# Experts' remainders of at most 64 rows in tiles of 320 rows, with column-halved output products

## The chip, the cores and the metric

The kernel runs on one core of a Trainium2 chip. The metric is device time in microseconds (us) of one launch; lower is better. Three runs of the kernel before gave 2270.71, 2273.41 and 2272.79 us (median 2272.79).

The engines are named as the profile names them: PE (TensorE matmul), PEld (its weight loads), DVE (VectorE), ACT (ScalarE), POOL (GpSimd) and SP (SyncE, which here only issues DMAs).

## The reference, cut to what matters

The input `x` has 4 images of 256 channels and 32x32 pixels. A first layer (normalisation, four small state-space scans, convolutions, attention, a projection) updates it; then each of the 4096 pixels is a token of 256 numbers that goes to two of eight experts. Only that second layer is touched by the change:

```python
top_w, top_i = jax.lax.top_k(gate_logits, TOP_K)          # TOP_K = 2 of 8 experts
top_w = jax.nn.softmax(top_w, axis=-1)
for e in range(E):
    h = jax.nn.gelu(xf @ W1[e] + b1[e], approximate=False)  # 256 -> 1024
    out = out + w_dense[:, e:e + 1] * (h @ W2[e] + b2[e])   # 1024 -> 256
```

There are 2 x 4096 = 8192 rows of work. Evaluated on its own inputs, the reference sends experts 0 to 7 these numbers of rows: 1024, 1065, 1023, 1012, 1006, 1048, 1041, 973. Divided by 256, that is 4, 4, 3, 3, 3, 4, 4, 3 full tiles and remainders of 0, 41, 255, 244, 238, 24, 17, 205 rows.

## The kernel before, in words

**Order of the whole.** The instruction order of all engines is written out by a hand-made scheduler: Python generators are advanced in ticks, and each `yield` gives way to the others. Image by image the first layer runs; when an image has passed it, `dispatch` normalises its tokens, picks the experts and scatters the rows into an array `XS` in device memory, in which each expert owns a region. Expert tiles (the generator `tiles()` and the class `Experts`) run beside the last image's convolutions and normalisations and then alone to the end.

**Tiles of rows.** A normal tile takes T = 256 rows of one expert. A wide tile (series WIDE = 3) takes 384: the last full 256 rows of an expert and the up to 128 rows that remain behind them. Which expert and which first row a tile has is computed on DVE from the counts (`wide_series`, `series`, `table`) and read into registers that address the DMAs. The code is laid out for the worst case: `SERIES = (8, 8, 19, 8)` tiles in four series. The last `LATE` = 7 normal tiles and the last `LATE_WIDE` = 4 wide ones stand in a conditional block behind everything else (`run`, line 2052) that is entered only if the counts need one of them. The tiles that always run are 8 + 8 + 12 normal and 4 wide. After the first 16 normal ones, the order is wide, normal, normal, normal, four times over.

**An expert must fit.** An expert whose remainder is at most 128 has it taken along by a wide tile; a larger remainder takes a padded normal tile of its own. Free wide slots take another expert's tile.

**One tile, step by step.** While tile n runs, tile n+1 is prepared. SP issues the DMA of its rows (`rows`, line 2069: `xs`, as 128-row blocks beside each other) and of its weights (`load`, lines 2095 to 2100: W1 and W2 in four pieces of 512 KB, biases). In the middle of tile n, behind its first output block, `front` turns the rows: PE transposes of 128x128 (line 2118, `xp`), a DVE copy out of PSUM (line 2121, `xT`), and four small DVE operations that make each row's weight and destination (lines 2126 to 2133). Then `tile` computes:

- the hidden layer, line 2149: 8 pieces of 128 hidden units, each two products (two halves of the 256 input channels) that stream `xT` past a piece of W1. Every fp32 product is two passes in the trace, so a tile has 32 matmul instructions of 256 columns, or of 384 in a wide tile;
- Gelu on ACT, line 2154, into `hs`;
- the output, line 2161: for each block of 128 rows, 8 products that hold 128 rows of `hs` as weights and stream W2 (256 columns), so 16 instructions of 256 columns a block. Two blocks share a PSUM tile, so that a wide tile's third block has one for itself;
- the bias on DVE (line 2170), the routing weight on DVE (line 2175), and one indirect DMA a block that adds the rows into `Y` (POOL, line 2181).

At the very end `bring_back` reads `Y`, transposes it and writes the output.

Of the kernel before, what the change touches and what calls it, by code (L numbers as in the profile page):

```python
# [9 lines left out]
F32 = mybir.dt.float32  # L10
# [35 lines left out]

LATE, LATE_WIDE = 7, 4


LOG_EXP = "natural_log_exp_and_others"
# [20 lines left out]
def network(  # L73
# [71 lines left out]
    with tc.tile_pool(name="w_conv", bufs=1) as wp, tc.tile_pool(  # L145
# [1149 lines left out]
        def tiles():  # L1295
# [45 lines left out]
            def rows(n):  # L1341
                s, i = order[n]
                xs[n] = act4.tile(
                    [P, experts.width(s) // P, experts.ROW], F32, tag="a4", name=f"xs_{n}"
                )
                experts.rows(s, i, tables[s], xs[n])

# [27 lines left out]
            for n in range(len(order)):  # L1375
                while n not in got or len(got[n]) == 4:
                    ahead(n, NHC)
                    yield 4
                if order[n] in ((0, 2), (1, 2)):
                    experts.count_up(order[n][0] + 1, temp)  # L1380
                if order[n] == (rest - 1, 2):
                    experts.count_up(wide, temp)
                while not T.get(("scanned",)):
                    yield 1
                while T.get(("hold",)):
                    T["held",] = True
                    yield 1
                s = order[n][0]
                pieces = 2 if s == wide else 1
                hs = [  # L1390
                    act8.tile(
                        [P, NHC // pieces, experts.width(s)], F32, tag="a8", name=f"hs_{n}_{k}"
                    ) for k in range(pieces)
                ]
                for at, _ in enumerate(experts.tile(
                    n, s, got[n], hs,
                    act4.tile([P, experts.width(s) // P, C], F32, tag="a4", name=f"ys_{n}"),
                )):
                    if at < 4:
                        loaded[0] = None  # L1400
                    ahead(n + 1, at)
                    yield T.get(("pace",), 1)
# [134 lines left out]
class Experts:  # L1537
# [10 lines left out]

    T = 256

    SERIES = (8, 8, 19, 8)
    WIDE = 3
    NT = N // P
    ROW = C + 4
# [2 lines left out]
    def __init__(self, ctx, tc, psum, B, b1, ident, eps5, ones_mean, Wg, bg, W1, W2, b2, out):  # L1557
# [3 lines left out]
        self.B = B  # L1561
        T, NT = self.T, self.NT
        NTOK = self.NTOK = B * N
        self.NTILE = max(NTOK * 2 // T + k - -(-k * (T // 2 + 1) // T) for k in range(NE + 1))
        PITCH = self.PITCH = NTOK + T + P
        self.SPARE = NE * PITCH
        md = ctx.enter_context(
# [298 lines left out]

    def width(self, s):

        return self.T + P if s == self.WIDE else self.T

    def follow(self, ins, others, reason):
        kind = mybir.DependencyInfo(
# [5 lines left out]
    def count_up(self, s, temp):  # L1878

        nc, K, n = self.nc, self.NTOK // self.T, self.SERIES[s]  # L1880
        steps = temp(f"steps_{s}", [P, NE, K])
        base = {self.WIDE: 0, self.WIDE - 1: self.T // 2}.get(s, self.T - 1)
        nc.gpsimd.iota(
            steps, [[0, NE], [self.T, K]], base=base,
            channel_multiplier=0, allow_small_or_imprecise_dtypes=True,
        )
        which = temp(f"which_{s}", [P, n, NE])
        nc.gpsimd.iota(
            which, [[1, n], [0, NE]], base=0, channel_multiplier=0,
            allow_small_or_imprecise_dtypes=True,  # L1890
        )
        self.numbers[s] = steps, which
# [131 lines left out]
    def run(self, tables):  # L2024

        tc, nc = self.tc, self.nc
        with tc.tile_pool(name="moe2", bufs=2) as m2:
            def load(v):
                return nc.values_load(
                    v[0:1, 0:1], min_val=0, max_val=sum(self.SERIES),  # L2030
                    skip_runtime_bounds_check_because="made from counts of at most NTOK rows",
                )

            def late_tile(s, i):
                j, W = f"{s}_{i}", self.width(s)
                w1 = m2.tile([P, NC2, DFF], F32, tag="w1", name=f"w1_{j}")
                w2 = m2.tile([P, NHC, C], F32, tag="w2", name=f"w2_{j}")
                got = self.load(
                    s, i, tables[s], [w1], [w2], m2.tile([P, C], F32, tag="b2", name=f"b2_{j}")
                )  # L2040
                xs = m2.tile([P, W // P, self.ROW], F32, tag="xs", name=f"xs_{j}")
                self.rows(s, i, tables[s], xs)
                got += self.front(
                    j, s, i, tables[s], xs, m2.tile([P, NC2, W], F32, tag="xT", name=f"xT_{j}")
                )
                for _ in self.tile(
                    j, s, got, [m2.tile([P, NHC, W], F32, tag="hs", name=f"hs_{j}")],
                    m2.tile([P, W // P, C], F32, tag="ys", name=f"ys_{j}"),
                ):
                    pass  # L2050

            with tc.If(load(self.any_late) > 0):
                for s, late in ((self.WIDE - 1, LATE), (self.WIDE, LATE_WIDE)):
                    n = self.SERIES[s]
                    with tc.If(load(self.used[s]) > 0):
                        for i in range(n - late, n):
                            late_tile(s, i)
            for b in range(self.B):
                self.bring_back(b, m2)

    def rows(self, s, i, table, xs):

        nc, tc, T = self.nc, self.tc, self.width(s)
        row = nc.values_load(
            table[1][0:1, 1, i : i + 1], engines=[mybir.EngineType.SP], min_val=0,
            max_val=self.SPARE,
            skip_runtime_bounds_check_because="made from counts of at most NTOK rows",
        )
        ins = nc.sync.dma_start(xs, self.XS[ds(row, T), :].rearrange("(t p) c -> p t c", p=P))
        if self.image_of(s) + 1 < self.B:  # L2070
            here = self.sent_by[self.image_of(s)]
            for other in self.sent[here:]:
                tc.declare_no_dep(ins.ins, other.ins, reason="full tiles of earlier images")
            self.read.append(ins)
        else:
            here = len(self.sent)
        if i == 0:
            self.follow(ins, self.sent[:here], "all rows are in")

    def load(self, s, i, table, w1, w2, b2_s):  # L2080

# [26 lines left out]
    def front(self, j, s, i, table, xs, xT):  # L2108

        nc, psum, m0, W = self.nc, self.psum, self.m0, self.width(s)  # L2110
        nt = W // P
        expert, _ = table
        each = NC2 if NC2 * W <= HALF else 1
        for c0 in range(0, NC2, each):
            xp = psum.tile([P, HALF], F32, tag="ps", name=f"xp_{j}_{c0}")
            for t in range(nt):
                for c in range(each):
                    nc.tensor.transpose(  # L2118
                        xp[:, ds(c * W + t * P, P)], xs[:, t, ts(c0 + c, P)], self.ident
                    )  # L2120
            nc.vector.tensor_copy(  # L2121
                xT[:, ds(c0, each), :].rearrange("p c t -> p (c t)"), xp[:, 0 : each * W]
            )

        late = m0.tile([P, 3, 1], F32, tag="late", name=f"late_{j}", bufs=2)[:, 0:nt]
        nc.vector.tensor_scalar(
            late, xs[:, :, C + 3 : C + 4], expert[:, i, :], None, ALU.is_equal
        )
        wgt = m0.tile([P, 3, 1], F32, tag="wgt", name=f"wgt_{j}", bufs=4)[:, 0:nt]
        nc.vector.tensor_tensor(wgt, late, xs[:, :, C + 2 : C + 3], ALU.mult)  # L2130
        nc.vector.tensor_tensor(wgt, wgt, xs[:, :, C + 1 : C + 2], ALU.add)
        dest = m0.tile([P, 3, 1], mybir.dt.int32, tag="dest", name=f"dest_{j}", bufs=4)[:, 0:nt]
        nc.vector.tensor_copy(dest, xs[:, :, C : C + 1])
        return [xT, wgt, dest]

    def tile(self, j, s, got, hs, ys):

        nc, psum, W = self.nc, self.psum, self.width(s)
        w1, w2, b2_s, b1_s, xT, wgt, dest = got
        nt, each, piece = W // P, max(1, HALF // W), NHC // len(hs)  # L2140

        def hidden(k):
            return hs[k // piece][:, k % piece, :]
# [1 line left out]
        for k0 in range(0, NHC, each):  # L2145
# [8 lines left out]
                nc.scalar.activation(hidden(k), hp[:, i, :], AF.Gelu, bias=b1_s[:, 0, k : k + 1])  # L2154
            if k0 % 2 == 0:
                yield
        for t in range(nt):
            if t % 2 == 0:
                yp = psum.tile([P, HALF], F32, tag="ps", name=f"y_{j}_{t}")
            for k in range(NHC):  # L2160
                nc.tensor.matmul(  # L2161
                    yp[:, ts(t % 2, C)], hidden(k)[:, ts(t, P)], w2(k),
                    start=(k == 0), stop=(k == NHC - 1),
                )
                if k % 4 == 3:
                    yield
            if t % 2 or t == nt - 1:
                t0 = t - t % 2
                some = t + 1 - t0
                nc.vector.tensor_tensor(  # L2170
                    ys[:, t0 : t + 1], yp[:, 0 : some * C].rearrange("p (t c) -> p t c", t=some),
                    b2_s.rearrange("p (a c) -> p a c", a=1).to_broadcast([P, some, C]), ALU.add,
                )
        for t in range(nt):
            nc.vector.tensor_scalar(ys[:, t, :], ys[:, t, :], wgt[:, t, :], None, ALU.mult)  # L2175

        added = []
        for t in range(nt):
            if t:
                nc.gpsimd.memset(self.apart, 0.0)  # L2180
            ins = nc.gpsimd.indirect_dma_start(  # L2181
                out=self.Y[:, :],
                out_offset=bass.IndirectOffsetOnAxis(ap=dest[:, t, :], axis=0),
                in_=ys[:, t, :], in_offset=None, compute_op=ALU.add,
            )
            for other in added:
                self.tc.declare_no_dep(ins.ins, other.ins, reason="no two share a row")
# [126 lines left out]
```

## Time and profile before

| | |
|---|---|
| median of three runs | 2272.79 us (2270.71 to 2273.41) |
| profiled execution, its own time | 2272.61 us |
| its span, first to last instruction | 2270.8 us |
| mean granted PE clock | 0.947 of full |
| PE busy | 2005.6 us (88%) |
| DVE / ACT / POOL busy | 1531.8 / 1234.5 / 1046.4 us |
| hidden layer of a normal tile (32 passes of 256 columns), last stretch | 6.91 us |
| hidden layer of a wide tile (32 passes of 384 columns) | 10.32 us |
| output of one block (16 passes of 256 columns) | 3.45 us |
| indirect adds into `Y` | 68 |

The span is cut into 40 slices for the busy shares; one slice is 56.8 us. A matmul row `128*64 128x512` gives the part of the array (rows x columns) that holds weights, then the moving operand (partitions x columns). PE is pipelined: the duration of one matmul is longer than the distance to the next, so costs are read from distances between starts.

### The profile page before, as it was taken

The page shows a single profiled execution, that of the slowest core. Times are in us where ns is not written, and L with a number is a line of the kernel's source. Part 1 is how long each engine was busy: PE and PEld are TensorE (multiplying, and loading weights), DVE is VectorE, ACT ScalarE, POOL GpSimd, SP SyncE. Part 2 cuts the span into 40 slices and gives each one's busy share as a digit, 9 for nine tenths or more (in the row PEclk, how much of TensorE's full clock was granted, in tenths as well). Part 3 has the DMA queues.
Part 4 walks back from the last instruction along what each step waited for, and adds up shares of the span by engine and source line. Part 5 has one row for each costly group of instructions (what it writes and reads, how often), then busy time and mean ns, then how long its engine had stood idle before and what let it go on. Part 6 is the DMA issues. An engine that isn't in the chain of part 4 may idle for free. (4 is left out here: it accounts for less than half of the span.)

```text
span 2270.8 us, 28249 instructions
## 1 busy us (share of the span) xinstructions
PE 2005.6 (88%) x8742; PEld 889.8 (39%) x8742; DVE 1531.8 (67%) x2211; ACT 1234.5 (54%) x2301; POOL 1046.4 (46%) x930
## 2 busy tenths in 40 slices
PE   6777878999987999987789999659999999999995
PEld 2111112322211332322123234116742677888884
DVE  3989998768899878789797977984245265111111
ACT  4665666678767666775746777325358432212221
POOL 0788888613688640576975034742040021422221
PEclk8889999999998999998899999789999999999997
DMA  3565553302453421244543013343240176866665
GB/s 100 142 155 121 124 137 89 99 10 69 100 128 93 98 48 38 76 106 108 144 99 86 20 45 82 80 151 96 91 117 1 45 215 167 245 186 181 169 160 160
DMA packets 156814, 248.78 MB, mean 110 GB/s; under 512 B 34596, under 2 KB 101700, under 8 KB 156520
## 3 DMA queue, kind: packets, MB, share of 16 engines
q1 hardware_dynamic: 136032, 220.59, 36.2%
q0 software_dynamic: 12976, 17.58, 4.0%
q10 hardware_dynamic: 7640, 8.65, 1.2%
q8 instruction: 72, 1.18, 0.2%
q14 instruction: 94, 0.77, 0.1%
HBM read 135.39 MB, written 35.84 MB: 75 GB/s over the span
## 5 line engine op out<-in xcount | busy, mean ns | idle before, releaser
L698 POOL TENSOR_TENSOR dA<-hs,cs 128x512 f32<-128x512 f32 x512 | 684.3, 1344 | 430.6 <-DVE hs L690 294.7
L669 ACT ACTIVATE dA<-dts,A 128x512 f32<-128x512 f32 x512 | 358.8, 717 | 162.6 <-DMA dts<-dt 96.9
L2181 POOL DMA_INDIRECT Y<-ys,dest x68 | 109.6, 1612 | 535.1 <-DVE ys L2175 528.3
L708 PE MATMUL yp<-dA,quads 128*32 128x512 f32 x1024 | 277.4, 639 | 79.7 <-POOL dA L698 68.9
L2154 ACT ACTIVATE hs<-h,b 128x256 f32<-128x256 f32 (+1 forms) x256 | 112.1, 484 | 387.6 <-PE h L2149 273.6
L1053 ACT ACTIVATE e<-st 128x512 f32<-128x512 f32 x512 | 263.7, 605 | 102.5 <-PE st L1043 83.3
L679 DVE TENSOR_TENSOR dBu<-dts,bs 128x512 f32<-128x512 f32 x384 | 259.9, 678 | 85.4 <-PE bs L661 24.5
L2149 PE MATMUL h<-xT,w 128*128 128x256 f32 (+1 forms) x1024 | 249.3, 400 | 14.3 <-DVE xT L2121 14.3
L2161 PE MATMUL y<-w,hs 128*128 128x256 f32 x1088 | 248.9, 381 | 5.0 <-ACT hs L2154 5.0
L690 DVE TENSOR_TENSOR_SCAN hs<-dA,last,dBu 128x512 f32<-128x512 f32 x192 | 243.6, 1269 | 4.7 <-ACT sq_lgn L1135 1.3
L690 DVE TENSOR_TENSOR_SCAN hs<-dA,dBu 128x512 f32<-128x512 f32 x192 | 231.7, 1207 | 11.5 <-issue 4.4
L1099 DVE TENSOR_TENSOR e<-e,e 128x512 f32<-128x512 f32 x256 | 169.9, 725 | 84.5 <-ACT e L1053 46.4
L2149 PEld LDWEIGHTS h<-xT,w 128*128 128x128 f32 x1024 | 197.6, 194 | 66.5 <-DVE xT L2121 16.0
L2161 PEld LDWEIGHTS y<-w,hs 128*128 128x128 f32 x1088 | 205.2, 191 | 38.9 <-issue 6.1
L661 PE MATMUL bs<-u,xpwT_s 128*32 128x512 f32 x1024 | 169.4, 671 | 55.3 <-DVE hs L690 24.8
L2121 DVE COPY xT<-xp 128x512 f32<-128x512 f32 (+1 forms) x36 | 23.4, 659 | 274.6 <-PE xp L2118 262.1
L1043 PE MATMUL st<-qk 32*128 32x512 f32 x1024 | 176.7, 643 | 4.2 <-DVE ys L2170 2.6
L708 PEld LDWEIGHTS yp<-dA,quads 128*32 128x32 f32 x1024 | 49.2, 113 | 287.7 <-POOL dA L698 186.8
L1089 PE MATMUL av<-e,v 128*32 128x512 f32 x1024 | 139.3, 609 | 0.0
L1043 PEld LDWEIGHTS st<-qk 32*128 32x128 f32 x1024 | 60.3, 184 | 120.0 <-issue 87.3
L1063 PE MATMUL av<-e,every 128*32 128x512 f32 x512 | 87.5, 601 | 3.7 <-DVE e L1099 3.7
L679 DVE TENSOR_TENSOR bs<-dts,bs 128x512 f32<-128x512 f32 x128 | 86.1, 672 | 1.9 <-DMA dts<-dt 1.9
(319 smaller groups left out, 2706.4 us busy)
## 6 DMA issues: line engine op xcount, KB each, us to landing
dts<-dt SPq DMA_DIRECT2D x512, 128.0 KB
w<-in_W_dram SPq DMA_DIRECT2D x124, 512.0 KB
cs<-cd SPq DMA_DIRECT2D x512, 64.0 KB
xd<-xn SPq DMA_DIRECT2D x64, 128.0 KB
xs<-XS SPq DMA_DIRECT2D x28, 260.0 KB
xn<-in_x_dram SPq DMA_DIRECT2D x8, 512.0 KB
XL<-xl SPq DMA_DIRECT2D x8, 512.0 KB
xl<-XL SPq DMA_DIRECT2D x4, 1024.0 KB
```

Source lines behind the costliest of these rows:

```text
L661: nc.tensor.matmul(bs[r], xpwT_s[:, n, s : s + 1].to_broadcast([P, 32]), T[b, n, "u"][:, half(h)], start=True, stop=True,)
L669: nc.scalar.activation(dA, T[b, n, h, "dts", g][:, 0, :], AF.Exp, scale=A[:, g, n, q : q + 1])
L679: nc.vector.tensor_tensor(dBu, T[b, n, h, "dts", g][:, 1, :], T[b, n, h, "bs", q], ALU.mult)
L690: nc.vector.tensor_tensor_scan(hs, T[b, n, h, "dA", i], dBu, 0.0 if h == 0 else last, ALU.mult, ALU.add)
L698: nc.gpsimd.tensor_tensor(dA, hs, T[b, n, h, "cs", q], ALU.mult)
L708: nc.tensor.matmul(T[b, n, h, "yp"][ts(g, 32)], quads, T[b, n, h, "dA", q * GD + g], start=False, stop=(q == GS - 1),)
L1043: nc.tensor.matmul(sts[i], k[r, ts(kt, P)], q[r, half(h)], start=True, stop=not shifted)
L1053: nc.scalar.activation(es[i], sts[i], AF.Exp, scale=1.0 / HD**0.5)
L1089: nc.tensor.matmul(accs[0][ts(i, HD)], v8[:, kt, ts(4 * g + i, HD)], es[i], start=(kt == 0), stop=(kt == NK - 1),)
L1099: nc.vector.tensor_tensor(first[i], first[i], es[i], ALU.add)
L2149: nc.tensor.matmul(hp[:, i, :], w1(c, k0 + i), xT[:, c, :], start=(c == 0), stop=(c == NC2 - 1))
L2161: nc.tensor.matmul(yp[:, ts(t % 2, C)], hidden(k)[:, ts(t, P)], w2(k), start=(k == 0), stop=(k == NHC - 1),)
```

## The change

Wide tiles shrink from 384 to 320 rows (`REST = 64`). A remainder of up to 64 rows rides in a wide tile, a larger one takes a padded normal tile. The worst case needs more normal tiles for that, so the series becomes 21 long and 9 of it stand in the conditional block; the tiles that always run keep their number and order. A list `blocks(s)` replaces the count `W // P`: a wide tile has blocks of 128, 128 and 64 rows.

For the 64-row block each step has a form of its own:

- `rows` issues two DMAs for a wide tile, the full blocks and the 64 rows;
- `front` transposes 64 rows against a 64x64 identity, and issues its four small DVE operations twice;
- in `tile` the eight output products hold 64 rows of `hs` as weights, so half of the array's columns. Even pieces k go to columns and PSUM partitions 0 to 63, odd ones to 64 to 127: two partial sums beside each other. ACT then copies the upper partial sum to a tile `other`, DVE adds the bias to it, and DVE adds it to the lower one;
- weighting and the indirect add handle 64 rows.

```diff
-LATE, LATE_WIDE = 7, 4
+LATE, LATE_WIDE = 9, 4
+REST = 64
-    SERIES = (8, 8, 19, 8)
+    SERIES = (8, 8, 21, 8)
-        return self.T + P if s == self.WIDE else self.T
+        return self.T + REST if s == self.WIDE else self.T
+    def blocks(self, s):
+        W = self.width(s)
+        return [(t, min(P, W - t * P)) for t in range(-(-W // P))]
...
-        base = {self.WIDE: 0, self.WIDE - 1: self.T // 2}.get(s, self.T - 1)
+        base = {self.WIDE: 0, self.WIDE - 1: REST}.get(s, self.T - 1)
...
-        ins = nc.sync.dma_start(xs, self.XS[ds(row, T), :].rearrange("(t p) c -> p t c", p=P))
+        full = T // P
+        got = [
+            nc.sync.dma_start(
+                xs[:, 0:full], self.XS[ds(row, full * P), :].rearrange("(t p) c -> p t c", p=P)
+            )
+        ]
+        if T % P:
+            got.append(
+                nc.sync.dma_start(xs[0 : T % P, full], self.XS[ds(row + full * P, T % P), :])
+            )
...
-            for t in range(nt):
+            for t, n in blocks:
                 for c in range(each):
                     nc.tensor.transpose(
-                        xp[:, ds(c * W + t * P, P)], xs[:, t, ts(c0 + c, P)], self.ident
+                        xp[:, ds(c * W + t * P, n)], xs[0:n, t, ts(c0 + c, P)],
+                        self.ident[0:n, 0:n],
                     )
...
+        for n, ts_ in ((P, slice(0, full)), (W % P, slice(full, nt))):
+            if n:
+                x = xs[0:n, ts_]
+                nc.vector.tensor_scalar(
+                    late[0:n, ts_], x[:, :, C + 3 : C + 4], expert[0:n, i, :], None, ALU.is_equal
+                )
...
-        for t in range(nt):
+        for t, n in blocks:
             if t % 2 == 0:
                 yp = psum.tile([P, HALF], F32, tag="ps", name=f"y_{j}_{t}")
+            parts = P // n
             for k in range(NHC):
                 nc.tensor.matmul(
-                    yp[:, ts(t % 2, C)], hidden(k)[:, ts(t, P)], w2(k),
-                    start=(k == 0), stop=(k == NHC - 1),
+                    yp[ts(k % parts, n), ts(t % 2, C)], hidden(k)[:, ds(t * P, n)], w2(k),
+                    start=(k < parts), stop=(k >= NHC - parts),
                 )
                 if k % 4 == 3:
                     yield
-            if t % 2 or t == nt - 1:
+            if parts > 1:
+                other = m0.tile([REST, C], F32, tag="other", name=f"other_{j}", bufs=1)
+                nc.scalar.copy(other, yp[n:P, 0:C])
+                nc.vector.tensor_tensor(other, other, b2_s[0:n], ALU.add)
+                nc.vector.tensor_tensor(ys[0:n, t], yp[0:n, 0:C], other, ALU.add)
+            elif t % 2 or t == len(blocks) - 1:
...
-                out_offset=bass.IndirectOffsetOnAxis(ap=dest[:, t, :], axis=0),
-                in_=ys[:, t, :], in_offset=None, compute_op=ALU.add,
+                out_offset=bass.IndirectOffsetOnAxis(ap=dest[0:n, t, :], axis=0),
+                in_=ys[0:n, t, :], in_offset=None, compute_op=ALU.add,
```

More of the change, by code (lines that the diff above doesn't have):

```diff
@@ L1343, in rows @@
                 xs[n] = act4.tile(
-                    [P, experts.width(s) // P, experts.ROW], F32, tag="a4", name=f"xs_{n}"
+                    [P, len(experts.blocks(s)), experts.ROW], F32, tag="a4", name=f"xs_{n}"
                 )
@@ L1396, in tiles @@
                     n, s, got[n], hs,
-                    act4.tile([P, experts.width(s) // P, C], F32, tag="a4", name=f"ys_{n}"),
+                    act4.tile([P, len(experts.blocks(s)), C], F32, tag="a4", name=f"ys_{n}"),
                 )):
@@ L1563, in __init__ @@
         NTOK = self.NTOK = B * N
-        self.NTILE = max(NTOK * 2 // T + k - -(-k * (T // 2 + 1) // T) for k in range(NE + 1))
+        self.NTILE = max(NTOK * 2 // T + k - -(-k * (REST + 1) // T) for k in range(NE + 1))
         PITCH = self.PITCH = NTOK + T + P
@@ L2040, in late_tile @@
                 )
-                xs = m2.tile([P, W // P, self.ROW], F32, tag="xs", name=f"xs_{j}")
+                xs = m2.tile([P, len(self.blocks(s)), self.ROW], F32, tag="xs", name=f"xs_{j}")
                 self.rows(s, i, tables[s], xs)
@@ L2047, in late_tile @@
                     j, s, got, [m2.tile([P, NHC, W], F32, tag="hs", name=f"hs_{j}")],
-                    m2.tile([P, W // P, C], F32, tag="ys", name=f"ys_{j}"),
+                    m2.tile([P, len(self.blocks(s)), C], F32, tag="ys", name=f"ys_{j}"),
                 ):
@@ L2068, in rows @@
         )
-        ins = nc.sync.dma_start(xs, self.XS[ds(row, T), :].rearrange("(t p) c -> p t c", p=P))
[L2070 to L2078, printed above, removed]
+        full = T // P
[8 more added lines that the diff above has]
+            )
+        for ins in got:
+            if self.image_of(s) + 1 < self.B:
+                here = self.sent_by[self.image_of(s)]
+                for other in self.sent[here:]:
+                    tc.declare_no_dep(ins.ins, other.ins, reason="full tiles of earlier images")
+                self.read.append(ins)
+            else:
+                here = len(self.sent)
+            if i == 0:
+                self.follow(ins, self.sent[:here], "all rows are in")
     def load(self, s, i, table, w1, w2, b2_s):
@@ L2110, in front @@
         nc, psum, m0, W = self.nc, self.psum, self.m0, self.width(s)
-        nt = W // P
+        blocks = self.blocks(s)
+        nt = len(blocks)
         expert, _ = table
@@ L2125, in front @@
         late = m0.tile([P, 3, 1], F32, tag="late", name=f"late_{j}", bufs=2)[:, 0:nt]
-        nc.vector.tensor_scalar(
-            late, xs[:, :, C + 3 : C + 4], expert[:, i, :], None, ALU.is_equal
-        )
         wgt = m0.tile([P, 3, 1], F32, tag="wgt", name=f"wgt_{j}", bufs=4)[:, 0:nt]
-        nc.vector.tensor_tensor(wgt, late, xs[:, :, C + 2 : C + 3], ALU.mult)
-        nc.vector.tensor_tensor(wgt, wgt, xs[:, :, C + 1 : C + 2], ALU.add)
         dest = m0.tile([P, 3, 1], mybir.dt.int32, tag="dest", name=f"dest_{j}", bufs=4)[:, 0:nt]
-        nc.vector.tensor_copy(dest, xs[:, :, C : C + 1])
+        full = W // P
+        for n, ts_ in ((P, slice(0, full)), (W % P, slice(full, nt))):
[4 more added lines that the diff above has]
+                )
+                nc.vector.tensor_tensor(
+                    wgt[0:n, ts_], late[0:n, ts_], x[:, :, C + 2 : C + 3], ALU.mult
+                )
+                nc.vector.tensor_tensor(
+                    wgt[0:n, ts_], wgt[0:n, ts_], x[:, :, C + 1 : C + 2], ALU.add
+                )
+                nc.vector.tensor_copy(dest[0:n, ts_], x[:, :, C : C + 1])
         return [xT, wgt, dest]
     def tile(self, j, s, got, hs, ys):
-        nc, psum, W = self.nc, self.psum, self.width(s)
+        nc, psum, m0, W = self.nc, self.psum, self.m0, self.width(s)
         w1, w2, b2_s, b1_s, xT, wgt, dest = got
-        nt, each, piece = W // P, max(1, HALF // W), NHC // len(hs)
+        blocks = self.blocks(s)
+        each, piece = max(1, HALF // W), NHC // len(hs)
         def hidden(k):
@@ L2173, in tile @@
                 )
-        for t in range(nt):
-            nc.vector.tensor_scalar(ys[:, t, :], ys[:, t, :], wgt[:, t, :], None, ALU.mult)
+        for t, n in blocks:
+            nc.vector.tensor_scalar(
+                ys[0:n, t, :], ys[0:n, t, :], wgt[0:n, t, :], None, ALU.mult
+            )
         added = []
-        for t in range(nt):
+        for t, n in blocks:
             if t:
```

## The prediction

> **What bounds the kernel now.** I read the page's parts first: PE is busy 88% of the span, and the chain that ended last is PE's, with the two expert products at its head. Then the stretches of the last 300 us: in each, PE is busy all the time, every other engine a quarter or less, the DMA engines about half to three quarters.
>
> ```profile
> PE   6777878999987999987789999659999999999995
> PE h L2149 9%; PE y L2161 8%; PE st L1043 2%; PE av L1089 1%; PE fc L396 1%; DVE xi L1237 1%; PE pr L396 1%; DMA Y<-ys,dest 1%; PE av L1063 1%; PE ao L396 1%; PE qkp L396 1%; PE fp L396 1%; POOL dA L698 1%; DVE hs L690 1%; PE xp L2118 1%
> ```
>
> ```profile
> 1975.83:1996.94 21.11, 21.11 (x85) 15.59 (x84) 3.22 (x9) 4.64 (x8) 3.23 (x3) 1.00 0.49 132
> 1996.94:2011.20 14.26, 14.26 (x70) 12.55 (x69) 2.44 (x9) 3.35 (x8) 5.03 (x5) 1.00 0.77 204
> 2104.01:2125.13 21.12, 21.12 (x85) 15.59 (x84) 3.23 (x9) 4.65 (x8) 3.23 (x3) 1.00 0.49 133
> 2231.64:2270.80 39.16, 12.02 (x67) 10.18 (x66) 6.68 (x12) 4.69 (x8) 3.23 (x3) 0.63 0.68 224
> ```
>
> The columns are the stretch, its length, then busy time (instructions) of PE, PEld, DVE, ACT and POOL, granted clock, DMA share and GB/s. The first and third stretch are wide tiles, the second a normal one; all four wide tiles take 21.1 us, at full clock. The third view is PE's timeline around a wide tile:
>
> ```profile
> 2099.90 0.82 PE L2118 MATMUL xp<-ident,xs 128*128 128x128 f32 x6
> 2100.56 3.62 PE L2161 MATMUL y<-w,hs 128*128 128x256 f32 x16
> 2104.01 10.48 PE L2149 MATMUL h<-xT,w 128*128 128x384 f32 x32
> 2114.34 3.62 PE L2161 MATMUL y<-w,hs 128*128 128x256 f32 x16
> 2117.79 0.60 PE L2118 MATMUL xp<-ident,xs 128*128 128x128 f32 x4
> 2118.22 7.07 PE L2161 MATMUL y<-w,hs 128*128 128x256 f32 x32
> ```
>
> No wait stands in any row: PE goes from one group to the next from 1947 to 2231.6 us. All four wide tiles lie in there, so what PE saves or pays in them moves the end one for one, as long as nothing else becomes late.
>
> **Which tiles run.** The 68 indirect adds are 28 x 2 + 4 x 3: no conditional tile ran. By the counts of the reference the remainders are 0, 41, 255, 244, 238, 24, 17, 205. None lies between 65 and 128, so both rules give the same tables: three experts need a wide tile, one free wide slot is filled, and padded whole tiles number 4 for each expert, 32 = 28 + 4. The tiles that run, and their order, stay; only the four wide ones get narrower.
>
> **Part 1, the hidden layer.** Starts 2104.01 to 2114.34 are 10.33 us for 32 passes of 384 columns, 323 ns each; 32 passes of 256 take 6.91 us, 216 ns. Halfway, 320 columns take 269 ns: 32 x 53.5 ns = 1.71 us less on PE a wide tile. ACT's Gelu is shorter too (0.58 us at 384 against 0.47 at 256), but ACT is busy 4.65 of 21.12 us.
>
> **Part 2, the third output block.** Before, 16 passes in 3.45 us. After, again 16 passes of 256 columns, with half-width weights on alternating column halves. If halves run beside each other, that is 8 slots of 216 ns = 1.73 us: 1.73 us less. If not, nothing is saved. The trace shows no pair of 64-column products, but quarters (qd, 128*32, accumulating like the new ones), with the start of a slot in each row:
>
> ```profile
> 1506.37 0.63 PE L2118 MATMUL xp<-ident,xs 128*128 128x128 f32 x4 [1.74 <-DMA xs<-XS]
> 1506.93 2.78 PE L866 MATMUL qd<-xm,qdwT_s 128*32 128x512 f32 x24
> ...
> 1507.38 1.04 PE L866 MATMUL qd<-xm,qdwT_s 128*32 128x512 f32 x8
> ...
> 1507.81 1.04 PE L866 MATMUL qd<-xm,qdwT_s 128*32 128x512 f32 x8
> ...
> 1507.38 0.13 PEld L866 LDWEIGHTS qd<-xm,qdwT_s 128*32 128x32 f32 x4 [0.30 <-issue]
> ```
>
> Four passes of 512 columns start every 0.43 us, which is what one full-width pass of 512 takes (four `fc` passes at 1774.25 take 1.71 us to the next start). So all four run beside each other and their loads overlap the streaming. I take full pairing. The nearest rows differ in one thing: their slots are 430 ns, the new ones 216. A 64-column load lies between the 110 ns of 32 columns and 190 ns of 128, about 137 ns, still below a slot; the bounds are 1.73 us and nothing.
>
> **Part 3, switching the array's division.** The gate products of the convolutions show what it costs to go from whole-array weights to another division and back:
>
> ```profile
> 1529.58 0.38 PE L2149 MATMUL h<-xT,w 128*128 128x256 f32 x1
> ...
> 1529.89 0.70 PE L880 MATMUL gp<-qs,qpwT_s 64*128 64x512 f32 x2
> ...
> 1530.43 0.59 PE L880 MATMUL gp<-qs,qpwT_s 64*128 64x512 f32 x2
> ...
> 1530.95 0.48 PE L2149 MATMUL h<-xT,w 128*128 128x256 f32 x1
> ...
> 1531.27 0.38 PE L2149 MATMUL h<-xT,w 128*128 128x256 f32 x1
> ```
>
> From 1529.58 to 1529.89 are 0.31 us where 0.216 is usual: 0.095 us lost. The first slot behind it is 0.54 instead of 0.43: 0.11 more, the load that could not be hidden. The way back loses 0.09 and again 0.105. With 32-column weights (qd) the second loss is 0.02 (0.45 against 0.43); behind an idle gap the first transpose's slot was longer by 0.03. A wide tile now has six switches: into and out of the half columns (0.14 and 0.20 us, the load of 64 columns put between), and, as the 64-row transposes hold weights on half of the array's rows, in and out for each of the two channel halves (0.125 three times, and 0.20 into the wide-array products): 0.92 us. Bounds: 6 x 0.09 = 0.54 and 6 x 0.20 = 1.2 us. The transposes themselves lose half of two slots of 0.109 us: 0.11 us saved.
> The Trainium skill, page TensorEngine Tiling (Array Packing), section Key Properties, says that changing the tiling mode drains TensorE. By that rule alone, with the 0.095 us above as the drain, the six switches would be 0.57 us and the whole change 1.4 us better than I sum; the measured refill behind the drain decides, so I keep 0.92.
>
> **Part 4, beside PE.** ACT gets a copy of 64x256 a wide tile (0.27 us for 128x128, 0.58 for 128x512: about 0.37), DVE two additions instead of one (0.42 each) and four more small ones (0.16 to 0.22 each). The bias lands some 0.8 us later, then weighting and the adds, before which POOL sat idle 17.3 us; DVE's next urgent work, the `xT` copy, comes ten us later, and the next tile's Gelus have 4 of 7 us free. Copies after Gelu show no table load at the kernel's end. If that cover were gone it would cost 0.8 us a wide tile. SP issues one more DMA of 0.38 us a wide tile, ahead of the next tile's W1; W1 issued at 2131.8 for a tile starting at 2139.4 leaves the tight 7.6 us, in normal tiles, which stay. The third add carries half of the rows. Tables of 21 instead of 19 tiles lengthen ten DVE operations by some 16 ns (0.31 us at 152 elements, 0.22 at 64), in front of the `xT` copy for which PE waits at 1931: 0.16 us paid. Code of two more conditional tiles is jumped over: nothing, as now.
>
> **Sum.** 1.71 + 1.73 + 0.11 - 0.92 = 2.63 us a wide tile, whose stretch of 21.12 becomes about 18.5; 4 x 2.63 - 0.16 = 10.4 us. The profiled execution of 2272.61 us becomes 2262.2; it lies 0.2 us below the median, so 2262.4 us.
>
> **Rivals.**
> 1. *The halves don't share the array.* If weights of one half can't be loaded while the other streams, a slot is 216 + 137 ns, the block 2.82 us and the time 4 x 1.1 = 4.4 us more: 2266.8. If the passes simply queue, 4 x 1.73 = 6.9 us more: 2269.3. Against it: the qd rows. For it: no row with slots as short. The Trainium skill, page TensorE: Matmul & The Clock Gate, Part 3, states that loads overlap running matmuls only where the row group differs; two column halves share all rows, so by that rule the first of these times would come. The quarter loads at 1507.38 ran beside their streams, so this trace disagrees.
> 2. *The gain turns into a wait.* PE is done with a wide tile 2.6 us sooner, and the next weights or rows are late: PE would show an idle gap, and 2268 to 2273 come out. Against it: 0.49 DMA share in wide stretches, and normal tiles that are fed in 14.26 us.
> 3. *Slower: conditional tiles run.* The stricter limit turns remainders of 65 to 128 into padded tiles. With one, whole tiles would number 33 and all nine late normal tiles would run: at least 9 x 14.26 = 128 us, so 2390 or more. It decides when expert 1, the nearest, has 65 rows left instead of 41, 24 more rows than the reference gives. Only a difference of arithmetic could do that.
> 4. *Slower by switching.* Switches must cost 0.60 us each, three times the dearest row, to eat 3.55 us.
>
> **How the numbers follow.** Forecast 0.74; rival 1 0.13, half at either time; rival 2 0.06; rivals 3 and 4 with unforeseen losses 0.07. The forecast's own range, with switches between their bounds (+1.5, -1.1 us) and runs scattering by 1.4 us, is 2259.5 to 2265. The low end is 2259, the high end 2269.5 to take in rival 1. A difference within 0.2% (4.5 us) can't be told from none; slower counts from 2277.3, faster up to 2268.2. So faster is the forecast, the half of rival 1 and a little: 0.81; same 0.12; slower 0.07.
>
> **What would show it.** The four wide stretches at 18.5 us without a gap; hidden passes 269 ns apart; half-column passes starting two by two every 216 ns; gaps of 0.31 us where the division changes; 68 indirect adds. I am wrong if the half-column block takes 2.8 us or more, if PE waits at a tile's first pass, or if more than 68 adds appear.

## The result and the profile after

The changed kernel took 2264.22 us (median of nine runs, 2258.32 to 2268.38), the one before beside it 2272.35 us (nine runs, 2269.51 to 2273.9): a ratio of 0.996, 95% interval 0.9949 to 0.9971, so 8 us or 0.4% faster. The forecast was 2262.4 in a range of 2259 to 2269.5. Two later comparisons, each on one chip, gave 2264.55 against 2274.62 (ratio 0.9953, 0.9941 to 0.9966) and 2259.76 against 2270.27 (0.9935, 0.9914 to 0.9956), about 10 us each.

The first interval, 6.6 to 11.6 us of gain, holds the other two.

The page's part on the chain that ended last, of the changed kernel: the two expert products still head it, with new line numbers.

```profile
PE h L2178 9%; PE y L2191 8%; PE st L1046 2%; PE av L1092 2%; PE fc L399 1%; DVE xi L1240 1%; PE pr L399 1%; DMA Y<-ys,dest 1%; PE av L1066 1%; PE xp L2137 1%; PE ao L399 1%; PE qkp L399 1%; PE fp L399 1%; POOL dA L701 1%; PE gate L1750 1%
```

The same stretches as before, a wide tile, the normal one behind it, and what follows the last product (stretch, length, busy time of PE, PEld, DVE, ACT, POOL, clock, DMA share, GB/s):

```profile
1979.43:1997.37 17.94, 17.94 (x86) 13.43 (x84) 3.23 (x9) 4.22 (x8) 3.24 (x3) 1.00 0.53 152
1997.37:2011.72 14.35, 14.35 (x70) 12.65 (x69) 2.85 (x10) 3.72 (x9) 4.90 (x5) 1.00 0.75 202
...
2224.51:2263.20 38.69, 11.94 (x67) 10.28 (x66) 6.69 (x12) 4.68 (x8) 3.23 (x3) 0.63 0.69 228
```

PE is still busy throughout the tiles; a wide stretch went from 21.12 to 17.94 us, the normal one behind it from 14.26 to 14.35, and the normal one ahead of it, in which the wide tile's rows are transposed, from 14.47 to 15.00. PE's timeline around a wide tile has no wait in it:

```profile
2036.33 1.15 PE L2137 MATMUL xp<-ident,xs 128*128 128x128 f32 x6
2037.42 3.72 PE L2191 MATMUL y<-w,hs 128*128 128x256 f32 x16
2040.97 8.78 PE L2178 MATMUL h<-xT,w 128*128 128x320 f32 x32
2049.59 3.62 PE L2191 MATMUL y<-w,hs 128*128 128x256 f32 x16
2053.04 0.60 PE L2137 MATMUL xp<-ident,xs 128*128 128x128 f32 x4
2053.48 5.50 PE L2191 MATMUL y<-w,hs 128*128 128x256 f32 x32
```

The hidden layer takes 8.62 us from start to start (10.33 before), the second and third output blocks together 5.43, to the start of the next hidden layer at 2058.91 (6.91 before). The six transposes, 0.66 us before, now take 1.09 (2036.33 to 2037.42); the timeline merges the two 64-row ones into the first row, and the third block into the last.

For the comparisons below I use one measure that leaves out all that runs ahead: the **stretch** from the hidden layer of the second normal tile ahead of the first wide one (the expectations call it the last) to the `any` product that follows the last output product. It was 284.54 us before (1947.10 to 2231.64) and is 274.33 (1950.18 to 2224.51): 10.21 us less. PE's timeline at its start, of the kernel before and of the changed one:

```profile
1947.10 7.07 PE L2149 MATMUL h<-xT,w 128*128 128x256 f32 x32
...
1950.18 7.07 PE L2178 MATMUL h<-xT,w 128*128 128x256 f32 x32
```

Other executions of the same two kernels have 284.64 and 274.44: in them PE waited 0.2 to 0.3 us just ahead of the stretch, and its first hidden layer then takes 0.1 us longer.

### The profile page after: what moved, and what is told of

Same layout as the page of the kernel before. It is cut to its first block, busy times and chain, and to the rows that moved or that the text cites. A ratio compares the mean times of both kernels' runs of the same rounds, so it can differ in the third digit from the quotient of the medians.

```text
span 2263.2 us, 28292 instructions
## 1 busy us (share of the span) xinstructions
PE 1997.6 (88%) x8742; PEld 881.5 (39%) x8742; DVE 1536.8 (68%) x2231; ACT 1234.4 (55%) x2305; POOL 1045.2 (46%) x930
## 5 line engine op out<-in xcount | busy, mean ns | idle before, releaser
L2178 PE MATMUL h<-xT,w 128*128 128x256 f32 (+1 forms) x1024 | 242.9, 394 | 14.5 <-DVE xT L2141 14.5
L2191 PE MATMUL y<-w,hs 128*128 128x256 f32 (+1 forms) x1088 | 243.1, 382 | 5.0 <-ACT hs L2183 5.0
L2191 PEld LDWEIGHTS y<-w,hs 128*128 128x128 f32 (+1 forms) x1088 | 197.3, 188 | 40.2 <-issue 7.5
```

Of the source, the lines that this page charges most:

```text
L2178: nc.tensor.matmul(hp[:, i, :], w1(c, k0 + i), xT[:, c, :], start=(c == 0), stop=(c == NC2 - 1))
L2191: nc.tensor.matmul(yp[ts(k % parts, n), ts(t % 2, C)], hidden(k)[:, ds(t * P, n)], w2(k), start=(k < parts), stop=(k >= NHC - parts),)
```

## The experiments

**1. Only one half of the columns.** Is it the pairing that shortens the third block?

```diff
-                    yp[ts(k % parts, n), ts(t % 2, C)], hidden(k)[:, ds(t * P, n)], w2(k),
-                    start=(k < parts), stop=(k >= NHC - parts),
+                    yp[0:n, ts(t % 2, C)], hidden(k)[:, ds(t * P, n)], w2(k),
+                    start=(k == 0), stop=(k == NHC - 1),
...
-                nc.scalar.copy(other, yp[n:P, 0:C])
-                nc.vector.tensor_tensor(other, other, b2_s[0:n], ALU.add)
-                nc.vector.tensor_tensor(ys[0:n, t], yp[0:n, 0:C], other, ALU.add)
+                nc.vector.tensor_tensor(ys[0:n, t], yp[0:n, 0:C], b2_s[0:n], ALU.add)
```

> All eight products of the 64-row block go to the same half of the columns, so no two of them can run beside each other; the copy on ACT and one addition on DVE fall away. Theory (the sum of the prediction): the third block needs 16 slots of 216 ns instead of 8, 1.73 us more a wide tile; the stretch of PE from the last normal tile's hidden layer ahead of the first wide tile to the last output product, 274.3 us in the changed kernel and 284.5 before, becomes 281.2, and the time is 6.9 us over the changed kernel's. Rival (the gain is the narrower hidden layer and lighter tails, pairing gives little): the stretch stays within 1 us of 274.3.

Measured: 2270.61 us beside 2264.55 of the changed kernel on the same chip, 6.1 us more; the stretch 281.32. The groups of instructions show the same 64 passes (four wide tiles), first of the changed kernel:

```profile
L2191 PE MATMUL y<-w,hs 128*64 128x256 f32 x64 | 7.8, 385 | 0.0
```

and of this one:

```profile
L2191 PE MATMUL y<-w,hs 128*64 128x256 f32 x64 | 14.7, 382 | 0.0
```

The time of one pass is the same (385 and 382 ns), the busy time 14.7 us instead of 7.8: without a partner on the other half the passes queue. Pairing is worth 6.9 us of the 10.2 (7.0 by the stretch, of which 0.1 comes from a wait just ahead of it). This kernel also leaves out a copy and an addition; the seventh experiment shows that the copy lies beside PE.

**2. Whole transposes.** What do the switches of the array's division cost? Rows and transposes as before, the products as changed.

```diff
-                        xp[:, ds(c * W + t * P, n)], xs[0:n, t, ts(c0 + c, P)],
-                        self.ident[0:n, 0:n],
+                        xp[:, ds(c * W + t * P, P)], xs[:, t, ts(c0 + c, P)], self.ident
...
+            nc.sync.dma_start(xs, self.XS[ds(row, T), :].rearrange("(t p) c -> p t c", p=P))
```

Here T is 384 rows again, and the four small DVE operations take all three blocks at once.

> The row reads and the transposes are those of before (one DMA of 384 rows, six whole-array transposes, four small DVE operations), the rest is the changed kernel; so four of the six switches of the array's division are gone. Theory (a switch costs drain and refill): the six transposes take 0.66 us instead of 1.08 and the next product's first slot is 0.10 shorter, 0.53 us a wide tile; the stretch of 274.3 becomes 272.2, the time 2.1 us less than the changed kernel's. Rival (a switch costs its drain alone, 0.09 us): 0.26 us a wide tile, the stretch 273.3.

Measured: the stretch 272.30 us, the time 2262.83 (2264.55 for the changed kernel in the same set, 2274.62 before; ratio to before 0.994, 0.9927 to 0.9953). PE's timeline of this kernel ahead of a wide tile:

```profile
2037.12 0.82 PE L2130 MATMUL xp<-ident,xs 128*128 128x128 f32 x6
2037.77 3.62 PE L2175 MATMUL y<-w,hs 128*128 128x256 f32 x16
2041.23 0.43 PE L2162 MATMUL h<-xT,w 128*128 128x320 f32 x1
```

The six transposes are back at 0.65 us, the 16 products behind them at 3.46 instead of 3.55. Saved are 0.53 us a wide tile, 2.0 to 2.1 in the stretch, as the theory asks; the rival's 273.3 did not come. That doesn't yet show the refill: the run takes out the switches and the 64-row transposes together, and the rival's 0.26 counts half a slot as saved by each of these transposes. Four drains of 0.09 us without that saving would be 0.37 us a wide tile, and the stretch 272.8. What the rest of the 0.53 is, rows of the changed kernel show further below. This version has the shortest stretch of all. Its time is the lowest of its set by 1.7 us, less than single runs of one kernel differ, so the stretch carries the verdict.

**3. The longer series alone.** The kernel before, wide tiles of 384 rows, with `SERIES = (8, 8, 21, 8)` and `LATE = 9`.

> The kernel before, with wide tiles of 384 rows and its own limit, but a series of 21 tiles of which 9 are conditional: only the longer tables and the longer conditional block. Theory: PE's wait ahead of 1931 us grows by 0.16 us, all else stays, 2272.6. Rival (the longer program or tables move what runs ahead of the expert tiles, as the changed kernel's profile, 2.8 us later at its first expert transpose, could suggest): 2274.5 to 2276.

Measured: 2274.87 us, which lies in the rival's range; but the kernel before took 2274.62 on this chip, so the ratio decides: 1.0002 (0.9992 to 1.0012). The stretch is 284.64, PE's idle time ahead of the hidden layer that waits for the tables 3.28 us, where the kernel before has 3.09 and the changed one 3.27. The wait is 3.09 to 3.12 us in all five profiles with the short tables, and 3.26 to 3.28 in six of the nine with longer ones; in two of the other three (2.21 and 2.31) the tile ahead ran 1 us longer, and the third, 3.18, is the fifth experiment. The tables cost some 0.18 us, and the time shows no more within its 0.1%: the theory holds.

**4. What runs ahead.** The profiled execution of the changed kernel was 2.8 us late at its first expert transpose (1509.18 against 1506.37), though the instructions up to there are the same. I ran it again, then the kernel before three times on another chip, then both beside each other on one chip.

> The changed kernel once more. Theory (the 2.8 us by which its profiled execution was late at the first expert transpose are scatter of the clock's low windows): another execution has this transpose anywhere from 1504 to 1511 us, and the stretch at 274.3 within 0.1. Rival (the change moves what runs ahead): the transpose at 1509 again, within 1 us, and the median 2264 again.

Measured: the transpose at 1510.75, the stretch 274.44, the median 2264.55. That tells the two apart poorly: 1.6 us from 1509, but late again.

> The kernel before, for another profile. So far the first expert transpose started at 1505.4 and 1506.4 us in the two profiles with 384-row tiles, and at 1506.4 and 1508.5 to 1510.8 in the seven with 320-row tiles, though the instructions ahead of it are the same. Theory (scatter of the clock's low windows): this profile and its two companions spread over 1505 to 1511. Rival (the change moves what runs ahead): all three lie under 1507.

> As the companion: the first expert transpose over 1507 in at least one of the three by the theory of scatter, under 1507 in all three by the rival.

> As the companion: the first expert transpose over 1507 in at least one of the three by the theory of scatter, under 1507 in all three by the rival.

Measured: transposes at 1508.99, 1509.89 and 1508.73, all over 1507, with the kernel before; the stretch 284.54 in all three. The three transposes lie within 1.2 us of each other, though, and do not spread as the theory had it. Their times are 2265.96, 2268.11 and 2265.57 us; all 22 runs of the kernel before on the chip of the first four experiments are above 2269.5, so the chip seems to matter.

> The kernel before and the changed one beside each other on one chip, for the one question that is left: whether the change moves what runs ahead of the expert tiles. This is the kernel before. Theory (scatter): its first expert transpose lies within 2 us of the changed kernel's, with either sign, and the times differ by the 10.1 us of the stretch, within 1.5 us. Rival (the change makes the part ahead some 3 us longer): the changed kernel's transpose is 2.5 us or more later, and the times differ by 7 us.

> The changed kernel beside the one before on one chip. Theory (scatter): first expert transpose within 2 us of the other's, time 10.1 us less, within 1.5 us, the stretch 274.3. Rival (the change makes the part ahead some 3 us longer): the transpose 2.5 us or more later, the time 7 us less.

Measured on one chip: 2259.76 us for the changed kernel; 2270.27 us for the kernel before over 17 runs, and 2272.27 for its companion copy. The difference of 10.5 us is within the theory's margin, 12.5 to the copy beyond it; the copy itself scattered from 2267.07 to 2280.63. The stretches are 274.44 and 284.64. PE's timelines at the first expert transpose, of the kernel before:

```profile
1508.43 0.63 PE L2118 MATMUL xp<-ident,xs 128*128 128x128 f32 x4 [1.53 <-DMA xs<-XS]
```

and of the changed kernel:

```profile
1504.71 0.63 PE L2137 MATMUL xp<-ident,xs 128*128 128x128 f32 x4 [1.88 <-DMA xs<-XS]
```

This time the changed one is 3.7 us earlier. That is more than the 2 us of the theory, so the scatter is larger than I had put it, but its sign is against the rival. What runs ahead scatters, whichever kernel it is.

The first expert transpose is not the place to look, however. Over all profiles it moves by 6.0 us, but the time from it to the start of the stretch by 14.2 (432.1 to 446.3), and most of that arises in one place, from the start of the fifth expert tile's hidden layer to that of the sixth, where PE also works on the attention products `st` and `av`. There the three profiles of the kernel before on one chip have 100.80 us each and no wait of PE. The eleven others have 105.7 to 112.4 us: 106.70 and 106.65 in the first profiles of the kernel before and of the changed one, 111.67 and 105.88 in the pair on one chip. In all eleven PE waits there, 1.2 to 5.4 us in sum (in the kernel before 2.64 us for DVE's `ys`), and the passes behind a wait are slower for some us. The granted clock 20 to 40 us behind the fifth tile's start is 1.00 in the three, 0.87 in the first profile of either kernel and 0.77 in the slower one of the pair; only the fifth experiment has waits there at a clock of 1.00. So low clock and waits come together, and why they come in some executions stays open.

**5. The limit at 32.** The price of the rival on the other side: what happens when one expert's remainder passes the limit? The tables send remainders over 32 to padded tiles (expert 1 has 41), with wide tiles unchanged. This kernel has ten conditional normal tiles where the changed one has nine, and it drops the declaration that the adds of one tile need not wait for each other.

```diff
-LATE, LATE_WIDE = 9, 4
+LATE, LATE_WIDE = 10, 4
-    SERIES = (8, 8, 21, 8)
+    SERIES = (8, 8, 22, 8)
...
-        base = {self.WIDE: 0, self.WIDE - 1: REST}.get(s, self.T - 1)
+        base = {self.WIDE: 0, self.WIDE - 1: REST // 2}.get(s, self.T - 1)
...
-            for other in added:
-                self.tc.declare_no_dep(ins.ins, other.ins, reason="no two share a row")
```

> The wide tiles stay at 320 rows, but the tables send every remainder over 32 to a padded tile, so that expert 1 with 41 counts as one too many: 33 whole tiles for 32 places, 10 conditional tiles (the worst case asks for one more), and the adds of one tile wait for each other. Theory (third rival of the prediction): the conditional block runs, all ten tiles of it, each at least the 14.26 us of a normal tile: 142 us or more on top of 2264, 2406 at the least; with weights loaded for only two tiles ahead in a new pool and no overlap of rows and products perhaps 20 to 25 us each, 2465 to 2515. Rival (only the tile that holds rows costs, the others are blank and quick): 2280 to 2290.

Measured in one execution: 2440.71 us, against 2273.12 for the kernel before on that chip. PE's timeline behind the last unconditional product:

```profile
2221.28 0.19 PE L1525 MATMUL any<-most,ones_mean 128*1 128x1 f32 x2
2241.79 1.08 PE L2137 MATMUL xp<-ident,xs 128*128 128x128 f32 x4 [20.32 <-DMA xs<-XS]
...
2261.47 7.17 PE L2178 MATMUL h<-xT,w 128*128 128x256 f32 x32 [0.94 <-DVE xT L2141]
...
2276.93 7.17 PE L2178 MATMUL h<-xT,w 128*128 128x256 f32 x32 [0.94 <-DVE xT L2141]
```

PE waits 20.3 us until the first rows are there. The first tile takes 17.8 us, each of the others 15.46 (2261.47 to 2276.93), blank or not; the adds number 88 instead of 68, so all ten conditional normal tiles ran. It is above the floor of 2406 and below the 2465 I thought likelier: no wait for weights shows, and of the 1.2 us by which such a tile is longer than a normal one, 0.94 is the wait for `xT`. From the `any` product to the end this kernel takes 217.5 us, the changed one 38.6; with nine tiles, as the changed kernel has them, a remainder over the limit would cost it some 163 us, an estimate from these rows.

**6. Short slots.** The one open point of rival 1 was that 216 ns slots might just hide a 137 ns load. Here the slots are halved.

```diff
...
+                elif k % 4 == 3:
+                    for i in range(NHC):
+                        nc.tensor.matmul(
+                            yp[ts(i % 2, n), ts(k // 4, P)], hidden(i)[:, ds(t * P, n)],
+                            w2(i)[:, ts(k // 4, P)], start=(i < 2), stop=(i >= NHC - 2),
+                        )
```

> The products of the 64-row block are cut into two halves of W2's columns: 32 passes of 128 columns in pairs, with twice as many weight loads. Theory (loads of one half run beside the streams of both): a pair every 109 ns, or, where the 137 ns load binds, every 137: 16 pairs in 1.75 to 2.2 us, so the block is at most 0.5 us longer than 1.73. Rival (a half's load must wait for the streams, which the 216 ns slots hid): a pair every 245 ns, 3.9 us.

Measured: the stretch 274.52 us (one execution: 2266.22). PE's timeline of the third block and the product behind it:

```profile
2056.66 1.97 PE L2198 MATMUL y<-w,hs 128*64 128x128 f32 x32
2058.56 2.64 PE L2178 MATMUL h<-xT,w 128*128 128x256 f32 x11
```

From start to start 1.90 us for 16 pairs; the changed kernel's block takes 1.88 (2057.03 to 2058.91). With the loss of 0.14 us at the edges taken off, a pair starts every 110 ns, although each has two loads, of 137 ns each in this trace. Twice as many loads cost next to nothing here: loads of one half overlap the streams of both.

**7. A slow join.** ACT copies the upper half four times.

> ACT copies the upper partial sum four times instead of once, so the join of the two halves is some 1.1 us later. Theory (the join lies beside PE): the stretch stays at 274.3 within 0.1 us. Rival (ACT or DVE holds up PE behind a wide tile): 1.1 us more a wide tile, 278.7.

Measured: the stretch 274.33 us, the changed kernel's to the hundredth (one execution: 2261.74). ACT's timeline shows the longer copy, and how close the next Gelu stands:

```profile
2055.46 1.57 ACT L2200 COPY other<-y 64x256 f32<-64x256 f32 x4 [8.73 <-PE y L2191]
2057.35 0.84 ACT L2183 ACTIVATE hs<-h,b 128x256 f32<-128x256 f32 x2 [0.32 <-PE h L2178]
```

The join lies beside PE: 1.2 us more of it move nothing.

## Why the prediction was right

**What bounds.** Right. PE has no gap in the stretch, and the experiments that changed its slots moved the stretch by what these add up to: 281.32 for 281.2, 272.30 for 272.2. (The fifth has 274.81, with a wait of 0.21 us of PE in it.) Some of the readings beside it were too round: behind the last product PE is busy 12.02 of 39.16 us only, and POOL is busy over a third of the normal stretch (5.03 of 14.26). The tightest place for DMA is not among the rows shown: the normal stretch ahead of the first wide tile has a DMA share of 0.99 before and 0.93 after, and PE doesn't wait there either.

**The hidden layer.** Forecast 1.71 us a wide tile, measured 10.33 - 8.62 = 1.71.

**The third block.** Full pairing, forecast from quarters with slots twice as long. The changed kernel's PE timeline, cut to the edges of the block:

```profile
2056.72 0.74 PE L2191 MATMUL y<-w,hs 128*128 128x256 f32 x3
...
2057.03 0.65 PE L2191 MATMUL y<-w,hs 128*64 128x256 f32 x4
...
2057.29 0.60 PE L2191 MATMUL y<-w,hs 128*64 128x256 f32 x4
...
2058.59 0.39 PE L2191 MATMUL y<-w,hs 128*64 128x256 f32 x2
...
2058.91 0.48 PE L2178 MATMUL h<-xT,w 128*128 128x256 f32 x1
```

From 2057.29 to 2058.59 seven pairs start in six steps of 216 to 217 ns. The switch in loses 0.09 (0.31 to the first pair) and 0.05 (its slot 0.26); the way out loses 0.10, and the first hidden slot another 0.10 (0.32 instead of 0.216). Forecast for both 0.34; measured 0.34. Rival 1 fell by this, and by the sixth experiment also where slots are shorter than a load. The rule behind it, from the Trainium skill's page TensorE: Matmul & The Clock Gate, Part 3, that loads overlap running matmuls only where the row group differs, is contradicted for column halves by these rows.

**The transposes.** Here a term was mis-sized. I gave half a slot saved for each 64-row transpose and 0.575 us for its switches, a net loss of 0.47 us. Measured are 1.09 - 0.66 = 0.43 in the transposes and 0.10 in the product behind them, 0.53:

```profile
2036.65 0.27 PE L2137 MATMUL xp<-ident,xs 64*128 64x64 f32 x1
2036.85 0.33 PE L2137 MATMUL xp<-ident,xs 128*128 128x128 f32 x1
2037.01 0.27 PE L2137 MATMUL xp<-ident,xs 128*128 128x128 f32 x1
2037.22 0.27 PE L2137 MATMUL xp<-ident,xs 64*128 64x64 f32 x1
2037.42 0.48 PE L2191 MATMUL y<-w,hs 128*128 128x256 f32 x1
2037.74 0.38 PE L2191 MATMUL y<-w,hs 128*128 128x256 f32 x1
```

A 64-row transpose takes 0.20 us from its start to the next start and pushes its own start to 0.20 behind the one before (2037.01 to 2037.22); a whole one takes 0.11. So a switch into a 64-row transpose loses 0.09; if the switch out of it loses as much, the 64-row transpose itself keeps a slot of 0.11, though it streams half as much. The whole transpose behind it takes 0.165 instead of 0.109, and the first product 0.32 instead of 0.216: 0.16 us more, the refill. Four switches of 0.093 are 0.37, and 0.37 and 0.16 are the 0.53. Read so, the switches cost a little less than the 0.575 that I gave, and it is the saving of 0.11 that did not come. The Trainium skill's page TensorEngine Tiling (Array Packing), Key Properties, names the drain alone; these rows show that the refill belongs to the price, 0.16 us of the 0.53 that the second experiment saved.

**The sum.** 1.71 + 1.73 - 0.34 - 0.53 = 2.57 us a wide tile against 2.63 forecast; four make 10.3, the stretch shows 10.21. The tables cost 0.18 for 0.16. Only the booking of the stretch was off: I expected 18.5 us in a wide stretch and found 17.94, because the transposes of a wide tile lie in the stretch ahead of it (0.53 us longer) and the first hidden slot behind its switch in the next (0.09 longer); 3.18 - 0.53 - 0.09 = 2.56 again.

**Beside PE.** Right as far as tried: the seventh experiment quadrupled ACT's copy without effect, and PE waits for no weights in the stretch. Rival 2 has nothing left. Rival 4 asked for switches of 0.60 us; the dearest is 0.20.

**The other side.** Rival 3 did not happen, 68 adds as before, and its price is now measured: 167.6 us over the kernel before on the same chip, from one whole tile more than the places hold. That was with ten conditional tiles; the forecast's floor of 128 us for nine was too low by the entry of 20 us, 1.2 us a tile and 2.4 more in the first.

**The median.** 2264.22 instead of 2262.4, inside the scatter of what runs ahead. Here luck had a part: the forecast is for a difference, and the absolute time depends on the executions and the chip, as the kernel before alone shows (2265 to 2274.6 us). The differences, 8.1, 10.1 and 10.5 us, are the better test of the 10.4 forecast.

## What to carry to other kernels

Where one engine is busy without gaps and the changed tiles lie inside that stretch, a sum of slots read from starts in the trace forecasts a change of half a per cent; compare versions by that stretch, not by single times. Two narrow products beside each other on column halves were worth it with 16 passes behind one switch, and a single narrow transpose was not: padding it to the whole array was cheaper. A size that is chosen to fit the data should be read with the price of not fitting beside it, here 10 us gained against 168 lost in the fifth experiment.

## What the runs showed of the hardware that I had not expected

- Loads of 64 columns take some 0.14 us, yet pairs of passes follow each other every 110 ns with a load for each pass.
- A 64x64 transpose between whole-array ones costs 0.20 us, nearly twice a whole one (0.11).
- With the same instructions, the part from the fifth to the sixth expert tile took from 100.80 to 112.4 us, and the kernel before ranged from 2265.09 us on one chip to a median of 2274.62 on another, while the stretch of either kernel agreed within 0.11 us everywhere.
